# Scores and weighted values of a block in two halves, other TensorE work between the halves, and masks with 32 rows

## The chip, the cores and the metric

One Trainium2 chip; the kernel is one program on one of its cores. The time is device microseconds of that core from start to end, the median of several runs. Lower is better. Engines are named as in the profile: PE is TensorE's matmuls, PEld its weight loads, DVE is VectorE, ACT is ScalarE, POOL is GpSimd, SP issues transfers.

## The reference

Two stages, each inside a layer norm with a residual. The first is an attention over 512 tokens (8 sequences) whose weights are a second-order Taylor expansion of the exponential. The second, which the change touches, is a small transformer of 6 layers:

```python
def attn_layer(x, Wqkv, qs, ksc, Wo):
    q, k, v = jnp.split(x @ Wqkv, 3, -1)          # 16 heads of 64
    q = l2norm(q) * qs
    k = l2norm(k) * ksc
    q = q * cos * scale + rotate_half(q) * sin * scale
    k = k * cos * inv + rotate_half(k) * sin * inv
    out = local_attention(q, k, v)
    return out @ Wo

def local_attention(q, k, v):                     # windows of 32 tokens
    bk2, bv2 = (look(bk), look(bv))               # the window and the one before it
    sim = jnp.einsum('bhwie,bhwje->bhwij', bq, bk2) * QK_SCALE
    sim = jnp.where(mask, -jnp.finfo(sim.dtype).max, sim)
    attn = jax.nn.softmax(sim, -1)
    return jnp.einsum('bhwij,bhwje->bhwie', attn, bv2)

for i in range(DEPTH):                            # 6
    x = attn_layer(shift_tokens(x), ...) + x
    x = ffn_layer(shift_tokens(x), ...) + x       # layer norm, gated GELU, 128 -> 2*341 -> 128
```

All is in float32; tokens are 128 numbers wide.

## The kernel before

**Tiling.** A unit of work is a *block*: 128 tokens (four windows) of one sequence in one layer. There are 6 layers x 8 sequences x 4 blocks = 192. The state of a sequence lies in SBUF by features, so that a projection is a matmul of a block's 128 columns of `state` with 512 columns of weights.

**Stages of a block.** The loop over `t` (line 703) is a pipeline written by hand: in round `t` the functions of block `t`, `t-1`, `t-2` and so on are called in a fixed order, `at(t, lag, step)` calling `step` on block `t - lag`. The steps of a block are:

- lag 0: `proj` for q and then k (two matmuls of 512 columns each, L421, into an `mm` tile in PSUM; VectorE multiplies with the rotary tables, L429 and L436; ScalarE squares both halves, L444; GpSimd adds, L454), `values` (two such matmuls, L481, copied by ScalarE, L482, and spread over windows by transfers into `v2`), `sum_squares` and `unit_length` (reciprocal norms; GpSimd multiplies them in, L470).
- lag 1: `by_features` in two calls (16 transposes of q and k in all; ScalarE copies them into `qT` and `kT`, L514), `scores`: two matmuls (L527) write the mask into both banks of the tile `sp`, and 64 small matmuls (L534: 64 rows, 32 columns of weights, 64 moving columns) add the scores of 16 heads and 4 windows. VectorE takes the maximum (L542), ScalarE does 16 exponentials (L546), VectorE sums them.
- lag 2: `by_keys` (8 transposes of the exponentials, copied into `pT`, L564), `weigh_values` (64 small matmuls, L574, into `po`; VectorE divides, L582), `out_by_features` (8 transposes, copied into `oT`, L596).
- lag 3: `out_project` (8 matmuls, L603, added to `state`, L608).

After the fourth block of a sequence, one step of the feed-forward layer is done in each of the next four rounds: `feed_norm` (4 transposes, layer norm), `feed_first` (4 transposes), `feed_middle` (6 matmuls, GELU, with table loads around it on ScalarE) and `feed_last` (3 matmuls). So of four rounds in a row each has another of these between its second half of `by_features` and its `scores`.

**What sets the order.** Only TensorE's order is fixed by hand (`manual_schedule` for PE, line 694). On the other engines a scheduler puts the instructions in an order when the kernel is built, by its own estimates and by priorities; `tc.high_priority()` stands around the copies out of the transposes, the maximum and the division. [...]

**PSUM.** Tag `mm` has two tiles of two banks, used in turn by q, k, v and the feed-forward matmuls; `tr` two tiles of one bank; `s` a single tile of two banks, which `sp` and `po` share. A new tile on a tag waits until every reader of the tile that it replaces is done. So v's projection waits for all that reads q's, its squares (L444) among it.

A float32 matmul appears in the trace as two records, each with its weight load; 64 small matmuls are 128 records of both kinds.

## Time and profile before

| what | value |
|---|---|
| median of 3 runs | 3888.19 us (3887.2 to 3889.86) |
| the profiled execution | 3893.85 us |
| its span from first to last instruction | 3892.1 us |
| mean granted TensorE clock | 0.99 |
| TensorE records (matmuls, and as many loads) | 65600 |
| second stage: first to last start of a score matmul (L534) | 565.7 to 3847.0 us |

A busy time on PE is not a rate: matmuls overlap, and their ends are modelled. Where the time goes is read from the chain of waits: it is followed back from the last instruction, at each step to what released it. A row such as "L574 PE MATMUL po<-v,pT 64\*32 64x64 f32 x24576 | 299.3, 225 | 44.7" is a group of instructions: line, engine, operation, what it writes from what, rows\*columns of weights, size of the output, number; then its busy time in us, the mean ns of one, and the idle time of the engine just before them with what ended it. In the timeline a row is start, duration, engine, line, operation and count, and in brackets what the engine waited for.

### The profile page before, as it was taken

The numbers are of one execution on the slowest core, as the hardware profiler recorded it, in microseconds if no ns is written. First come the engines' busy times: TensorE is split into PE (matmuls) and PEld (weight loads), VectorE is DVE, ScalarE is ACT, GpSimd is POOL, SyncE is SP. The second block draws the span as 40 slices with busy tenths as digits, with TensorE's granted clock in tenths as the row PEclk, the third lists the DMA queues.
The fourth block names the chain that finished last, engine by engine and source line by source line (L and its number), as shares of the span: only waits on it lengthen the run. The fifth ranks groups of instructions, "written<-read, shape, count | busy, mean of one in ns | idle before, by whom it ended". The sixth has DMA issues, their size and how long they took to land.

```text
span 3892.1 us, 149565 instructions
## 1 busy us (share of the span) xinstructions
PE 3729.8 (96%) x65600; PEld 2474.2 (64%) x65600; DVE 2818.2 (72%) x4300; ACT 2657.5 (68%) x6745; POOL 1837.0 (47%) x1311
## 2 busy tenths in 40 slices
PE   8999989999999999999999999999999999999997
PEld 4555456666666666666666666666666666666665
DVE  4555567777867777777777777777787777777775
ACT  5565656776767777777777677777677777766664
POOL 0000025555555555555555555555555555555552
PEclk9999999999999999999999999999999999999998
DMA  2000012222222222222222322223222222222221
GB/s 81 17 9 12 6 50 71 59 66 60 76 74 63 63 63 66 71 75 65 60 62 64 82 65 66 65 56 82 70 66 59 66 65 56 65 68 68 64 67 37
DMA packets 153208, 233.46 MB, mean 60 GB/s; under 512 B 32622, under 2 KB 53356, under 8 KB 151788
## 3 DMA queue, kind: packets, MB, share of 16 engines
q1 hardware_dynamic: 152556, 223.89, 22.4%
q8 instruction: 517, 8.47, 0.9%
q14 instruction: 135, 1.11, 0.1%
HBM read 24.54 MB, written 4.19 MB: 7 GB/s over the span
## 4 chain that ended last, share of the span: by engine, by line
PE 89%; ACT 5%; issue 3%; DVE 2%; DMA 0%; POOL 0%; POOLq 0%; DVEq 0%; SPq 0%; ACTq 0%
PE tr L70 17%; PE mm L421 17%; PE mm L481 9%; PE py L603 9%; PE sp L534 7%; PE po L574 6%; PE y L282 4%; PE mm L625 3%; PE py L657 3%; PE mm L626 3%; PE sc L252 2%; PE sp L527 2%; ACT sq L444 2%; PE vv L230 2%; PE po L318 2%
## 5 line engine op out<-in xcount | busy, mean ns | idle before, releaser
L454 POOL TENSOR_TENSOR qk<-t,t 128x1024 f32<-128x1024 f32 x384 | 909.2, 2368 | 999.6 <-DVE t L436 999.5
L421 PE MATMUL mm<-wqkv,state 128*128 128x512 f32 x1536 | 727.1, 596 | 3.7 <-ACT v L482 2.6
L470 POOL TENSOR_TENSOR qk<-qk,ss 128x1024 f32<-128x1024 f32 x384 | 722.3, 1902 | 16.0
L429 DVE TENSOR_TENSOR t<-mm,tab 128x512 f32<-128x512 f32 x768 | 497.8, 685 | 242.8 <-PE mm L421 231.3
L546 ACT ACTIVATE pe<-sp,mx 128x64 f32<-128x64 f32 x3072 | 651.4, 376 | 27.6 <-DVE mx L542 27.3
L436 DVE TENSOR_TENSOR t<-mm,tab 128x1024 f32<-128x1024 f32 x384 | 465.9, 1213 | 0.0
L457 DVE TENSOR_REDUCE ss<-sq 128x16 f32<-128x1024 f32 x384 | 461.9, 1203 | 2.0 <-ACT sq L444 2.0
L444 ACT ACTIVATE sq<-mm 128x512 f32<-128x512 f32 x768 | 422.6, 610 | 47.2 <-DVE t L436 45.6
L603 PEld LDWEIGHTS py<-oT,wo 128*128 128x128 f32 x3072 | 374.8, 193 | 93.5 <-issue 56.2
L70 PEld LDWEIGHTS tr<-ident,qk 128*128 128x128 f32 x3072 | 345.7, 141 | 127.1 <-issue 105.7
L70 PE MATMUL tr<-ident,qk 128*128 128x128 f32 x3072 | 412.1, 277 | 7.4 <-ACT qT L514 2.3
L596 ACT COPY oT<-tr 128x512 f32<-128x512 f32 x384 | 207.3, 589 | 266.2 <-PE tr L70 265.2
L421 PEld LDWEIGHTS mm<-wqkv,state 128*128 128x128 f32 x1536 | 264.1, 192 | 191.6 <-issue 188.0
L481 PE MATMUL mm<-wqkv,state 128*128 128x512 f32 x768 | 367.9, 602 | 16.8 <-ACT sq L444 16.8
L603 PE MATMUL py<-oT,wo 128*128 128x128 f32 x3072 | 376.0, 276 | 1.0 <-ACT oT L596 0.9
L582 DVE TENSOR_TENSOR on<-po,su 128x1024 f32<-128x1024 f32 x192 | 235.1, 1224 | 170.1 <-PE po L574 170.1
L534 PEld LDWEIGHTS sp<-kT,qT 64*32 64x32 f32 x24576 | 271.9, 106 | 116.7 <-issue 113.8
L574 PE MATMUL po<-v,pT 64*32 64x64 f32 x24576 | 299.3, 225 | 44.7 <-issue 44.7
L482 ACT COPY v<-mm 128x1024 f32<-128x1024 f32 x192 | 194.5, 1013 | 211.0 <-PE mm L481 211.0
L534 PE MATMUL sp<-kT,qT 64*32 64x64 f32 x24576 | 312.2, 227 | 26.0 <-issue 25.2
L574 PEld LDWEIGHTS po<-v,pT 64*32 64x32 f32 x24576 | 258.5, 105 | 86.4 <-issue 86.2
L542 DVE TENSOR_REDUCE mx<-sp 128x16 f32<-128x1024 f32 x192 | 234.6, 1222 | 106.9 <-PE sp L534 106.3
(108 smaller groups left out, 5171.0 us busy)
## 6 DMA issues: line engine op xcount, KB each, us to landing
v<-v SPq DMA_DIRECT2D x1152, 128.0 KB
v<-v SPq DMA_DIRECT2D x672, 64.0 KB
wqkv<-in_L_ffn_Wqkv_dram SPq DMA_DIRECT2D x6, 1536.0 KB
wo<-in_L_ffn_Wo_dram SPq DMA_DIRECT2D x6, 512.0 KB
xin<-_attn_hidden_states_dram SPq DMA_DIRECT2D x8, 256.0 KB
xr<-_attn_hidden_states_dram SPq DMA_DIRECT2D x8, 256.0 KB
x<-xr SPq DMA_DIRECT2D x8, 256.0 KB
xr<-x SPq DMA_DIRECT2D x8, 256.0 KB
```

The source lines that it names most:

```text
L70: nc.tensor.transpose(ps[:cols, :rows], src, ident[:rows, :rows])
L421: nc.tensor.matmul(ps[:, a].rearrange("p h d -> p (h d)"), lhs, wqkv[:, s, a, :], start=True, stop=True)
L429: nc.vector.tensor_tensor(t2[:, a], ps[:, 1 - a], tab[:, 2 * s + 1, j, HF * a : HF * (a + 1)].unsqueeze(1).to_broadcast([P, H, HF]), ALU.mult,
L436: nc.vector.tensor_tensor(t1, ps, tab[:, 2 * s, j, :].rearrange("p (a d) -> p a d", a=2).unsqueeze(2) .to_broadcast([P, 2, H, HF]), ALU.mult,)
L444: nc.scalar.activation(sq[:, :, a, :], ps[:, a], AF.Square)
L454: nc.gpsimd.tensor_tensor(qk[:, s].rearrange("p h a d -> p a h d"), t1, t2, ALU.add)
L470: nc.gpsimd.tensor_tensor(t, t, ss[:, i, :].unsqueeze(2).to_broadcast([P, H, HD]), ALU.mult)
L481: nc.tensor.matmul(ps[:, p, :], lhs, L["wqkv"][:, 2, p, :], start=True, stop=True)
L534: nc.tensor.matmul(sp[W * w : W * (w + 1), p, pair, :], qT[HD * p : HD * (p + 1), pair, W * w : W * (w + 1)], kT[HD * p : HD * (p + 1), pa ...
L546: ex = nc.scalar.activation(pe[:, pair, p, :], sp[:, p, pair, :], AF.Exp, bias=mx[:, p, pair : pair + 1])
L574: nc.tensor.matmul(po[W * w : W * (w + 1), p, pair, :], pT[r, pair, W * w : W * (w + 1)], v2[r, w, HD * pair : HD * (pair + 1)], start=Tru ...
L603: nc.tensor.matmul(py, L["wo"][:, c, :], oT[:, c, :], start=(c == 0), stop=(c == NP - 1))
```

## The change

Four things are edited.

1. `scores` and `weigh_values` take a half (4 of 8 pairs of heads) and are called twice a round; their ends (maximum and exponentials, division) become `softmax` and `divide`. Between the halves of the scores TensorE now has `out_by_features` and half of the next block's q projection; between the halves of the weighing it has half of v's projection and the first half of `by_features`.
2. `proj` is cut into `project` (one matmul of 512 columns) and `turn` (the work of the other engines), so that a half of a projection can stand alone. The first half of v's projection comes before the weighing, the second within it.
3. The next block's layer is looked up, and loaded if it is new, near the end of the round before.
4. `each` holds, in rows 0 to 31 and again in rows 32 to 63, four 32x32 identities side by side. With it the mask of a block is written by a matmul of 32 rows, taken from rows 0 to 31 for one bank and 32 to 63 for the other. Blocks that begin a sequence keep the 128-row form with `mask0`.

```diff
@@ -65,6 +65,13 @@
 
     mask = const.tile([P, 2 * W], BF16, tag="mask", name="mask")
     mask0 = const.tile([P, 2 * W], BF16, tag="mask0", name="mask0")
+
+    each = const.tile([2 * W, P], BF16, tag="each", name="each")
+    for a in range(2):
+        for w in range(4):
+            nc.vector.tensor_copy(
+                each[W * a : W * (a + 1), W * w : W * (w + 1)], ident[W * a : W * (a + 1), W * a : W * (a + 1)]
+            )
 
     def transposed(ps, src, rows, cols):
         nc.tensor.transpose(ps[:cols, :rows], src, ident[:rows, :rows])
@@ -406,21 +413,25 @@
 
         return dict(wqkv=wqkv, wo=wo, w1=w1, w2=w2, tab=tab)
 
-    def proj(u, s):
+    def project(u, s, half):
+
+        lhs = state[u["b"]][:, u["j"] * P : (u["j"] + 1) * P]
+        if half == 0:
+            u["proj", s] = psum.tile([P, 2, 512], F32, tag="mm", name="mm")
+        nc.tensor.matmul(
+            u["proj", s][:, half, :], lhs, u["L"]["wqkv"][:, s, half, :], start=True, stop=True
+        )
+
+    def turn(u, s):
 
         L, b, j = u["L"], u["b"], u["j"]
-        wqkv, tab = L["wqkv"], L["tab"]
-        lhs = state[b][:, j * P : (j + 1) * P]
+        tab = L["tab"]
         if s == 0:
             u["ss"] = f2.tile([P, 2, H], F32, tag="ss", name="ss")
             u["qk"] = f2.tile([P, 2, H, 2, HF], F32, tag="qk", name="qk")
         ss, qk = u["ss"], u["qk"]
 
-        ps = psum.tile([P, 2, H, HF], F32, tag="mm", name="mm")
-        for a in range(2):
-            nc.tensor.matmul(
-                ps[:, a].rearrange("p h d -> p (h d)"), lhs, wqkv[:, s, a, :], start=True, stop=True
-            )
+        ps = u.pop(("proj", s)).rearrange("p a (h d) -> p a h d", d=HF)
         sq = f2.tile([P, H, 2, HF], F32, tag="sq", name="sq")
         t1 = f2.tile([P, 2, H, HF], F32, tag="t1", name="t1")
         t2 = f2.tile([P, 2, H, HF], F32, tag="t2", name="t2")
@@ -472,14 +483,10 @@
             )
 
     def values(u):
-        L, b, j = u["L"], u["b"], u["j"]
-        lhs = state[b][:, j * P : (j + 1) * P]
+        j = u["j"]
 
         v0 = f3.tile([P, 2, 512], F32, tag="v0", name="v0")
-        ps = psum.tile([P, 2, 512], F32, tag="mm", name="mm")
-        for p in range(2):
-            nc.tensor.matmul(ps[:, p, :], lhs, L["wqkv"][:, 2, p, :], start=True, stop=True)
-        nc.scalar.copy(v0, ps)
+        nc.scalar.copy(v0, u.pop(("proj", 2)))
 
         v2 = f2.tile([P, 4, 512], F32, tag="v2", name="v2")
         for p in range(2):
@@ -516,19 +523,23 @@
             B_["kT"] = f2.tile([P, NP, W + P], F32, tag="kT", name="kT")
             nc.gpsimd.tensor_copy(B_["kT"][:, :, :W], u["kT"][:, :, P:])
 
-    def scores(u):
+    def scores(u, half):
 
         qT, kT = u["qT"], u["kT"]
 
 
-        mk = mask0 if u["j"] == 0 else mask
-        sp = psum.tile([P, 2, NP, 2 * W], F32, tag="s", name="sp", bufs=1)
-        for p in range(2):
+
+        if half == 0:
+            u["sp"] = psum.tile([P, 2, NP, 2 * W], F32, tag="s", name="sp", bufs=1)
+        sp = u["sp"]
+        for p in range(2) if half == 0 else ():
+            r = slice(W * p, W * (p + 1))
+            lhs, mk = (identb, mask0) if u["j"] == 0 else (each[r], mask[r])
             nc.tensor.matmul(
-                sp[:, p], identb, mk.unsqueeze(1).to_broadcast([P, NP, 2 * W]),
+                sp[:, p], lhs, mk.unsqueeze(1).to_broadcast([lhs.shape[0], NP, 2 * W]),
                 start=True, stop=False, skip_group_check=True,
             )
-        for pair in range(NP):
+        for pair in range(NP // 2 * half, NP // 2 * (half + 1)):
             for w in range(4):
                 for p in range(2):
                     nc.tensor.matmul(
@@ -537,6 +548,10 @@
                         kT[HD * p : HD * (p + 1), pair, W * w : W * (w + 2)],
                         start=False, stop=True, skip_group_check=True,
                     )
+
+    def softmax(u):
+
+        sp = u.pop("sp")
         mx = f2.tile([P, 2, NP], F32, tag="mx", name="mx")
         with tc.high_priority():
             nc.vector.tensor_reduce(mx, sp, AX.X, ALU.max, negate=True)
@@ -563,20 +578,25 @@
             with tc.high_priority():
                 nc.scalar.copy(pT[:, c : c + 4, :], ps)
 
-    def weigh_values(u):
-
-        v2, pT, su = u["v2"], u["pT"], u["su"]
-        po = psum.tile([P, 2, NP, HD], F32, tag="s", name="po", bufs=1)
-        for pair in range(NP):
+    def weigh_values(u, half):
+
+        v2, pT = u["v2"], u["pT"]
+        if half == 0:
+            u["po"] = psum.tile([P, 2, NP, HD], F32, tag="s", name="po", bufs=1)
+        for pair in range(NP // 2 * half, NP // 2 * (half + 1)):
             for w in range(4):
                 for p in range(2):
                     r = slice(HD * p, HD * (p + 1))
                     nc.tensor.matmul(
-                        po[W * w : W * (w + 1), p, pair, :],
+                        u["po"][W * w : W * (w + 1), p, pair, :],
                         pT[r, pair, W * w : W * (w + 1)],
                         v2[r, w, HD * pair : HD * (pair + 1)],
                         start=True, stop=True,
                     )
+
+    def divide(u):
+
+        po, su = u.pop("po"), u["su"]
         u["on"] = on = f1.tile([P, NP, 2, HD], F32, tag="on", name="on")
         with tc.high_priority():
             dv = nc.vector.tensor_tensor(
@@ -701,30 +721,35 @@
         for k in range(len(steps) + 2):
             slot(k)
         for t in range(len(units) + 7):
-            if t < len(units):
-                u = units[t]
-                if u["l"] not in layers:
-                    layers[u["l"]] = load_layer(u["l"])
-                u["L"] = layers[u["l"]]
 
 
             gelus = 0 <= t - 5 < len(units) and units[t - 5]["j"] == NB - 1
             if gelus:
                 gelu_only()
-            at(t, 0, proj, 0)
+            if t == 0:
+                units[0]["L"] = layers[0]
+                at(t, 0, project, 0, 0)
+            at(t, 0, project, 0, 1)
+            at(t, 0, turn, 0)
             at(t, 3, out_project)
-            at(t, 0, proj, 1)
+            at(t, 0, project, 1, 0)
+            at(t, 0, project, 1, 1)
+            at(t, 0, turn, 1)
             at(t, 2, by_keys)
 
             if t == 0:
                 head_norm(NG - 1)
+            at(t, 0, project, 2, 0)
+            at(t, 2, weigh_values, 0)
+            at(t, 0, project, 2, 1)
             at(t, 0, values)
             if t == 1:
                 attn_out(B - 1)
             if t == 3:
                 to_state(B - 1)
             at(t, 1, by_features, 0)
-            at(t, 2, weigh_values)
+            at(t, 2, weigh_values, 1)
+            at(t, 2, divide)
             at(t, 0, sum_squares, 1)
             if not gelus:
                 at(t, 0, unit_length)
@@ -735,8 +760,16 @@
             if gelus:
                 at(t, 0, unit_length)
             at(t, 6, feed_last, ends=True)
-            at(t, 1, scores)
+            at(t, 1, scores, 0)
             at(t, 2, out_by_features)
+            if t + 1 < len(units):
+                u = units[t + 1]
+                if u["l"] not in layers:
+                    layers[u["l"]] = load_layer(u["l"])
+                u["L"] = layers[u["l"]]
+                at(t + 1, 0, project, 0, 0)
+            at(t, 1, scores, 1)
+            at(t, 1, softmax)
 
 
 def _rotary(n):
```

## The prediction

> **What bounds the kernel now.** I read the page first (busy times, the chain), then the chain of waits in a stretch of the middle, then the timeline of single blocks, and last what single lines wait for.

> ```profile
> PE 3729.8 (96%) x65600; PEld 2474.2 (64%) x65600; DVE 2818.2 (72%) x4300; ACT 2657.5 (68%) x6745; POOL 1837.0 (47%) x1311
> PE 89%; ACT 5%; issue 3%; DVE 2%; DMA 0%; POOL 0%; POOLq 0%; DVEq 0%; SPq 0%; ACTq 0%
> L574 PE MATMUL po<-v,pT 64*32 64x64 f32 x24576 | 299.3, 225 | 44.7 <-issue 44.7
> q8 instruction: 517, 8.47, 0.9%
> ```

> TensorE makes 89% of the chain that ends last; "issue" is 3% of 3892 us, 117 us. The chain of waits says where that is: inside the two groups of small matmuls.

> ```profile
> 2038.31 0.87 PE tr L70 x8
> 2039.18 1.22 PE po L574 x76
> 2040.40 1.09 issue
> 2041.49 0.43 PE po L574 x24
> ...
> 2056.26 0.87 PE tr L70 x8
> 2057.14 1.72 PE mm L481 x4
> 2058.86 0.87 PE tr L70 x8
> 2059.73 1.42 PE po L574 x91
> 2061.15 1.02 PE tr L70 x8
> ```

> The upper weighing stops for 1.09 us in its middle with no semaphore behind it; the lower runs through in 1.42. A group is 128 loads and 128 matmuls; 8.47 MB of instruction transfers in 517 packets are 16.4 KB each, and for TensorE's 131200 records that is 254 records to a packet. So a group eats about one packet in 1.4 us. These stops, an average 117/192 = 0.61 us a block, are all the idle time there is to win: a block takes (3847.0-565.7)/191 = 17.18 us by the first and last start of L534.

> The other thing to see is what TensorE's third projection (L481) waits for, in a block with a table load (first five lines) and in an ordinary one:

> ```profile
> 2033.89 1.28 ACT L82 ACT_TABLE_LOAD   x1
> 2034.98 1.04 PE L70 MATMUL tr<-ident,pe 128*128 128x128 f32 x8
> 2035.19 1.09 ACT L444 ACTIVATE sq<-mm 128x512 f32<-128x512 f32 x2
> 2036.16 1.08 ACT L564 COPY pT<-tr 128x512 f32<-128x512 f32 x2
> 2036.33 1.98 PE L481 MATMUL mm<-wqkv,state 128*128 128x512 f32 x4 [0.31 <-ACT sq L444]
> ...
> 2055.38 1.09 ACT L444 ACTIVATE sq<-mm 128x512 f32<-128x512 f32 x2 [0.39 <-DVE t L436]
> 2056.10 1.04 PE L70 MATMUL tr<-ident,pe 128*128 128x128 f32 x8
> 2056.74 1.08 ACT L564 COPY pT<-tr 128x512 f32<-128x512 f32 x2 [0.27 <-PE tr L70]
> 2056.97 1.88 PE L481 MATMUL mm<-wqkv,state 128*128 128x512 f32 x4
> ```

> L481 takes the `mm` buffer that the q projection filled, so it may start only when ScalarE has squared both halves of q. In the upper block the squares end at 2036.28 and the matmul starts at 2036.33. In the lower one they end at 2056.47, half a microsecond before TensorE gets there. That half microsecond is the slack on which everything below turns.

> [...] eight transposes occupy 0.87 us before a projection and 1.02 after a weighing. [...] in the first stage eight 32-row records of 384 columns (L252) take 0.86 us, where four full-height records of 512 take 1.91. [...] from 1070 to 1095 us, where TensorE stopped for over 3 us, the granted clock is 0.86, and a q projection lasts 3.41 us instead of 1.88.

> **The change part by part**, per block, in the profiled execution.

> 1. The stops for instructions. Between the halves of the scores now lie eight transposes and half a projection (0.9 + 0.86 us), between the halves of the weighing half a projection and eight transposes: 256 instructions now last over 2.5 us instead of 1.4. I take all of it as gone: -0.61. (Bounds: -0.4 to -0.61.)

> 2. Two more small groups. From the 1.37 us of 114 uninterrupted records (last one 0.22 long) a record takes 10.2 ns, so a half takes 0.65 and the leaving costs 0.15 (1.02 - 0.87); entering costs 0.10 (transposes before a weighing start 0.97 apart from it, 2058.69 to 2059.66, not 0.87). A split adds 0.10 + 0.15[...]: 0.2, two of them +0.4. (0.2 to 0.6.)

> 3. Masks with 32 rows: two matmuls of 0.215 beside each other save 0.215 in three of four blocks (mask0 keeps 128 rows)[...]: -0.12 on average. (-0.16 to +0.05.) The eight small copies that make `each` lie at the start, on VectorE, beside loads: nothing.

> 4. The order on ScalarE. This decides. Nobody wrote it; in the built program it has changed. Before, a block runs: 16 exponentials, both squares of q, both copies of pT, copy of v, and so on (142 of 192 blocks; with a table load behind the exponentials in 46 more). In the changed program those 142 run: 16 exponentials, first square of q, **both copies of pT, second square of q**, both squares of k, qT, kT, copy of v. The 46 run: exponentials, table load, both copies of pT, then all four squares. The first half of v's projection still waits for the second square of q (its semaphore's value is that instruction's), and the pT copies wait for TensorE's transposes of pe. So TensorE finishes those transposes, and has to wait until ScalarE has copied them and then squared q. Behind the waiting matmul stand both weighings, the second half of v, the transposes of q and k, the feed-forward step and the scores.

> Ordinary block, from the first transpose of pe: the eighth ends at 1.04, the second pT copy starts at about 1.08, the square 0.48 later (1.56; two take 1.08), ends 0.60 later (2.16), the matmul starts 0.05 later: 2.21 to 2.24. Without the wait it starts at 0.87. Wait: **1.37**. It cannot be hidden: TensorE's own transposes begin it.

> Table-load block, from the last score matmul: maximum 0.25 to 1.47 (a 1.22 row), exponentials from 1.51 for 3.39 to 4.90, table to 6.20, two copies 1.0 to 7.18, two squares to 8.26, matmul 8.3. TensorE, free of waits, would be there after leaving 0.15, half of q 0.86, L603 1.78, k 1.72 and transposes 0.87: 5.38. Wait 2.93; such a block had 0.47 before: +2.46.

> Block after the feed-forward norm (one of four): its second ScalarE step (exponential of ln_rs) now stands behind both oT copies, which wait for transposes behind the first half of the scores, and VectorE's four xn (0.32 each) all stand ahead of the maximum, where two did. The maximum then starts 0.9 late, and with it the exponentials: wait 2.2 instead of 1.37.

> Smaller: the late start reloads weights, 0.1 in three of four blocks (L481 lasts 1.98 after a wait, 1.88 without); the squares of k now precede the qT copies and wait for VectorE, so the second transposes of q and k start about 0.1 late; the xn transposes wait some 0.3 longer.

> Sum over four blocks: waits 1.37 + 2.2 + 2.46 + 1.37 = 7.4; reloads and late transposes 0.3 + 0.4 + 0.3 = 1.0; splits +1.6; masks -0.5; stops -2.4. Together **+7.1 us per four blocks**, for 48 such fours +341 us. The profiled execution is 3893.85 us; 4235 follows. The median of runs is 5.7 us lower, 4229. To this comes the clock: the 2.9 us waits stand in 46 blocks, and a half-clock window of 3.4 us costs up to 1.7 us; with a sixth of that, some 13 us, I forecast **4240 us**, 9% slower.

> What is moved beside this: loading a layer is issued a third of a block earlier on SP and POOL, with buffers free for a layer: nothing. Half of q earlier: its buffer was read by the squares of k, done 5 us before: nothing. The v copy comes one weighing half later; its transfers are used two blocks on, and have over 20 us: nothing.

> **Rivals.**
> - Faster: the wait is short, because the q buffer is in truth free early and TensorE stays the bound as now. Then -0.61 + 0.4 - 0.12 = -0.33 a block, -63 us: **3825**. For it speaks that L481 waits only 45.9 us in all now (below); against it that the order and the semaphore are in the built program. It decides if the second square of q ends before TensorE's last pe transpose. 7%.
> - Half the wait: ScalarE gets ahead, table-load blocks wait 1.5 and the norm block as others do, splits cost little: four blocks +3.5, +168 us: **4056**. 9%.
> - The clock falls in most table-load blocks and in the norm blocks: 90 windows of 1.2 us, +108 us over 4229: **4337**. 9%.
> - Nothing measurable: stops won and waits lost cancel; it needs waits of 0.3 a block: 3888. 1%.

> ```profile
>   ACT sq L444: 45.9, 93
> ```

> **How the numbers follow.** The forecast has 74%; its own range, from the bounds of the stops, splits and clock and 0.15 us either way on each wait, is 4160 to 4310. For eight in ten I widen it downward and upward: 4110 to 4330. This measurement tells about 0.2% from no change. Slower by more than that: forecast, half wait, clock, 92%; same 1%; faster 7%.

> **What would show it.** Right: the first v matmul of a block (new L421 behind pe transposes) waits for ScalarE's squares (L455), about 1.4 us in most blocks, near 3 in a quarter of them, some 300 us or more in all; the issue share falls to 1% or less; TensorE's busy share falls below 90%; mask pairs start together. Wrong: L421 waits less than 100 us for L455; or "issue" keeps its 3%, and then point 1 fails; or splits show groups of over 0.9 us a half.

## The result, and the profile after

The changed kernel takes **4355.96 us** (median of 4 runs, 4354.68 to 4358.46) against 3887.69 (4 runs, 3883.25 to 3889.86) for the kernel before on the same chip: a ratio of 1.1207, 95% interval 1.1187 to 1.1226. The profiled execution is 4355.78 us with a span of 4354.0, 462 us more than before.

The page of the changed kernel first: the busy times, and the chain that ended last, by engine.

```profile
PE 3947.2 (91%) x65600; PEld 2474.5 (57%) x65600; DVE 2787.1 (64%) x4308; ACT 2637.6 (61%) x6745; POOL 1843.1 (42%) x1311
...
PE 61%; ACT 26%; DVE 10%; issue 2%; DMA 0%; ACTq 0%; POOL 0%; POOLq 0%; DVEq 0%; SPq 0%
```

The same 65600 matmuls, but TensorE's part of the chain has fallen from 89% to 61%, and ScalarE's has risen from 5% to 26%. The mean granted clock is 0.971 where it was 0.99. What TensorE waits for (a line, who lets it go, us in total, times, longest), in the kernel before and in the changed one:

```profile
PE po L574 <- issue: 44.7, 62, 2.1
PE sp L534 <- issue: 25.2, 25, 3.6
PE mm L481 <- ACT sq L444: 16.8, 46, 2.2
PE tr L70 <- ACT qT L514: 14.2, 48, 0.8
```

```profile
PE mm L421 <- ACT sq L455: 323.6, 192, 2.8
PE tr L77 <- ACT qT L521: 17.2, 50, 0.8
...
PE sp L545 <- issue: 4.4, 3, 2.4
```

In all 192 blocks the first half of v's projection waits for ScalarE's squares of q. The stops inside the small groups, which the list puts down to issue and the prediction to instructions, 44.7 and 25.2 us in the kernel before, are 4.4 in the scores and below every row of this list in the weighing. The chain of waits in an ordinary block gives the mechanism piece by piece (start, length, what):

```profile
2041.75 0.81 ACT pe L561 x3
2042.56 0.49 ACT sq L455
2043.05 0.96 ACT pT L579 x2
2044.01 0.51 ACT sq L455
...
2044.56 1.13 PE mm L421 x2
```

Before v starts, the path runs on ScalarE: the last exponentials, a square of q, both copies of pT, and only then the other square. In the kernel before this stretch of the chain was TensorE's own. A block with a table load shows what such a wait does to the rest (timeline: start, length, engine, line, operation; in brackets the idle time before and what ended it):

```profile
3411.57 1.28 ACT L89 ACT_TABLE_LOAD   x1
3412.86 1.07 ACT L579 COPY pT<-tr 128x512 f32<-128x512 f32 x2
3413.82 1.11 ACT L455 ACTIVATE sq<-mm 128x512 f32<-128x512 f32 x2
3414.98 1.13 PE L421 MATMUL mm<-wqkv,state 128*128 128x512 f32 x2 [2.79 <-ACT sq L455]
...
3417.02 2.07 PE L421 MATMUL mm<-wqkv,state 128*128 128x512 f32 x2
3418.89 1.50 PE L77 MATMUL tr<-ident,qk 128*128 128x128 f32 x8
```

After an idle stretch of 2.79 us the half projection at 3417.02 lasts 2.07 us instead of 1.12, and the eight transposes 1.50 instead of 1.04. That is not a wait: the granted clock is 0.77 in the 4 us from 3418 on and 1.00 in the 8 us from 3400 on (windows of time: length; busy time and count of five engines; granted clock; DMA share; GB/s).

```profile
3418.00:3422.00 4.00, 4.00 (x82) 3.08 (x81) 0.78 (x1) 2.19 (x4) 0.70 (x2) 0.77 0.00 0
3400.00:3408.00 8.00, 7.67 (x224) 5.42 (x223) 4.16 (x4) 4.29 (x9) 5.39 (x5) 1.00 0.46 111
```

Counted over the trace, TensorE runs at half clock for 253.6 us, in 68 stretches, 62 of them of 3.41 us; before it was 77.2 us in 16, 12 of them of 3.41 us. Half of the difference, 88 us, is my estimate of the time lost, if TensorE has work throughout.

The idle times of the list are short of the delays, because the modelled end of one group lies behind the start of the next: eight transposes last 1.04 us, and the matmul behind them starts 0.87 after they do. So I count from the start of each group of TensorE to the start of the next, over the second stage. The transposes of the exponentials, behind which v waits, take 191.1 us before and 547.3 after. The 462 us then have these parts:

- the wait before v: +356;
- the two splits, 0.36 us a block each: +138;
- half clock, by the length of the groups that run in it: about +72;
- smaller terms, above all the longer first matmuls of v after a wait: under +10;
- the 32-row masks: about -14;
- the stops that are gone: about -97, more than the 70 of the list, which leaves out gaps under 0.15 us.

The experiments test the main ones.

### The profile page after: what moved, and what is told of

It reads as the page before. It is cut to its first block, busy times and chain, and to the rows that moved or that the text cites. A ratio compares the mean times of both kernels' runs of the same rounds, so it can differ in the third digit from the quotient of the medians.

```text
span 4354.0 us, 149387 instructions
## 1 busy us (share of the span) xinstructions
PE 3947.2 (91%) x65600; PEld 2474.5 (57%) x65600; DVE 2787.1 (64%) x4308; ACT 2637.6 (61%) x6745; POOL 1843.1 (42%) x1311
## 3 DMA queue, kind: packets, MB, share of 16 engines
q8 instruction: 517, 8.47, 0.8%
## 4 chain that ended last, share of the span: by engine, by line
PE 61%; ACT 26%; DVE 10%; issue 2%; DMA 0%; ACTq 0%; POOL 0%; POOLq 0%; DVEq 0%; SPq 0%
PE mm L421 15%; ACT pe L561 12%; PE tr L77 11%; PE sp L545 6%; PE po L590 6%; DVE mx L557 5%; ACT sq L455 4%; ACT pT L579 4%; PE y L289 3%; PE mm L645 3%; PE mm L646 3%; PE py L677 3%; PE sc L259 2%; PE vv L237 1%; PE sp L538 1%
## 5 line engine op out<-in xcount | busy, mean ns | idle before, releaser
L421 PE MATMUL mm<-wqkv,state 128*128 128x512 f32 x2304 | 1269.4, 648 | 326.3 <-ACT sq L455 323.6
L481 POOL TENSOR_TENSOR qk<-qk,ss 128x1024 f32<-128x1024 f32 x384 | 722.2, 1902 | 16.0
L455 ACT ACTIVATE sq<-mm 128x512 f32<-128x512 f32 x768 | 462.3, 636 | 404.8 <-DVE t L447 404.8
L421 PEld LDWEIGHTS mm<-wqkv,state 128*128 128x128 f32 x2304 | 375.8, 197 | 507.4 <-ACT sq L455 368.2
L440 DVE TENSOR_TENSOR t<-mm,tab 128x512 f32<-128x512 f32 x768 | 509.2, 684 | 80.3 <-PE tr L77 74.9
L77 PEld LDWEIGHTS tr<-ident,qk 128*128 128x128 f32 x3072 | 355.6, 145 | 145.3 <-issue 114.3
L590 PEld LDWEIGHTS po<-v,pT 64*32 64x32 f32 x24576 | 279.5, 111 | 197.0 <-issue 196.7
L590 PE MATMUL po<-v,pT 64*32 64x64 f32 x24576 | 346.0, 235 | 0.0
L545 PE MATMUL sp<-kT,qT 64*32 64x64 f32 x24576 | 334.7, 226 | 4.4 <-issue 4.4
L521 ACT COPY qT<-tr 128x512 f32<-128x512 f32 x384 | 232.4, 605 | 51.6 <-PE tr L77 51.6
```

Of the source, the lines that this page charges most:

```text
L77: nc.tensor.transpose(ps[:cols, :rows], src, ident[:rows, :rows])
L421: nc.tensor.matmul(u["proj", s][:, half, :], lhs, u["L"]["wqkv"][:, s, half, :], start=True, stop=True)
L440: nc.vector.tensor_tensor(t2[:, a], ps[:, 1 - a], tab[:, 2 * s + 1, j, HF * a : HF * (a + 1)].unsqueeze(1).to_broadcast([P, H, HF]), ALU.mult,
L455: nc.scalar.activation(sq[:, :, a, :], ps[:, a], AF.Square)
L481: nc.gpsimd.tensor_tensor(t, t, ss[:, i, :].unsqueeze(2).to_broadcast([P, H, HD]), ALU.mult)
L545: nc.tensor.matmul(sp[W * w : W * (w + 1), p, pair, :], qT[HD * p : HD * (p + 1), pair, W * w : W * (w + 1)], kT[HD * p : HD * (p + 1), pa ...
```

## The experiments

My theory after the comparison: (1) v waits because a square of q stands behind the copies of pT in ScalarE's order, (2) the long waits bring half clock, which costs time of its own, (3) each split costs more than I had put on it. The rivals are that the wait comes from splitting itself, since ScalarE's whole path is too long however it is ordered; that the clock is only a companion of the waits; that the splits are nearly free and the waits explain all. The ratio behind each time is against the kernel before, measured beside it on the same chip; two runs from different chips are compared by their times and by their ratios.

**Both squares of q ahead of the copies.** The changed kernel, with one constraint on ScalarE's order (`issue_behind(a, b)` puts `a` behind `b` on their engine):

```diff
-            nc.scalar.activation(sq[:, :, a, :], ps[:, a], AF.Square)
+            squares_of[s] = nc.scalar.activation(sq[:, :, a, :], ps[:, a], AF.Square)
...
-                nc.scalar.copy(pT[:, c : c + 4, :], ps)
+                issue_behind(nc.scalar.copy(pT[:, c : c + 4, :], ps), squares_of[0])
```

> The change, with one thing put back: both squares of q stand ahead of the pT copies on ScalarE, as in the kernel before. Theory ORDER (the wait before v's first half comes from ScalarE's order): exponentials end 4.8 us after the last score matmul, two squares end at 5.7, the matmul starts at 5.8 instead of 6.9; so a wait of 0.4 instead of 1.5 in ordinary blocks, and about 1 us less in the two other kinds. 48 x (4 x 1.05) = 200 us less, and some 50 us less of half clock: about 4100 us. Theory PATH (even in the old order maximum, exponentials and squares are longer than TensorE's work after the second half of the scores) says that a wait for the squares of 0.4 to 2 us stays in every block and that the kernel stays slower than the one before. Theory SPLITS (the doubled small groups cost it): no change, over 4300 us.

Measured: 4152.55 us (4148.03 to 4158.59), ratio 1.0665 (1.0646 to 1.0684), clock 0.991. One constraint takes 203 us off the changed kernel (211 by the two ratios). Its waits:

```profile
PE mm L422 <- ACT sq L456: 141.0, 191, 2.2
PE tr L77 <- ACT qT L522: 49.7, 85, 1.9
```

The idle time before v falls by 183 us, but 191 waits stay, and 33 us come back before transposes of q and k (49.7 for 17.2). Half clock falls to 79 us. So the order is the largest single cause, not the only one.

**The same order given to the kernel before.** Nothing of the change; only a square of q placed behind the copies of pT:

```diff
-            nc.scalar.activation(sq[:, :, a, :], ps[:, a], AF.Square)
+            squares_of[s] = nc.scalar.activation(sq[:, :, a, :], ps[:, a], AF.Square)
...
-                nc.scalar.copy(pT[:, c : c + 4, :], ps)
+                copy = nc.scalar.copy(pT[:, c : c + 4, :], ps)
+        if 0 in squares_of:
+            issue_behind(squares_of.pop(0), copy)
```

> The kernel before in everything, TensorE's order too, save that the second square of q stands behind both pT copies on ScalarE, as in the changed kernel. ORDER alone: v's first matmul comes 2.2 us after the first transpose of pe instead of 0.87 in 142 blocks (+190 us), about 0.9 us later than now in the 46 with a table load (+43 us), the stretches stay under 1.4 us idle so that the clock stays[...]: about 4080 us. If the order is harmless without the halves: 3888 us.

Measured: 4099.76 us (4095.52 to 4102.04), ratio 1.0519 (1.0504 to 1.0534). Without a split and without masks, the order alone costs the kernel before 202 us against the runs beside it (median 3897.68). What TensorE waits for, and in the timeline v's projection in a block without table load:

```profile
PE mm L482 <- ACT sq L445: 238.1, 192, 2.2
PE sp L535 <- issue: 19.2, 20, 3.6
...
PE po L577 <- issue: 2.9, 7, 1.1
```

```profile
2042.72 1.99 PE L482 MATMUL mm<-wqkv,state 128*128 128x512 f32 x4 [1.23 <-ACT sq L445]
```

The wait is 1.23 us, where the kernel before had none. The 202 us are what is left of a larger loss: by the starts of groups the wait costs 245 us, and the weighing is 49 us shorter, because its stops are gone (2.9 us where they were 44.7). So here the stops went with a wait ahead of the group, without any split.

**What the rest of the waiting is.** In the run with the order mended, the first half of the scores stands ahead of the transposes and of half of q, the second half behind them, so the maximum and the exponentials begin later than q's squares would like. Here only the transposes are left between the halves:

```diff
             at(t, 1, scores, 0)
             at(t, 2, out_by_features)
+            at(t, 1, scores, 1)
+            at(t, 1, softmax)
             if t + 1 < len(units):
...
                 at(t + 1, 0, project, 0, 0)
-            at(t, 1, scores, 1)
-            at(t, 1, softmax)
```

> The change with both squares of q ahead of the pT copies, and with only the eight transposes between the halves of the scores; both halves of q follow the second. PATH: what is left of the loss with the old order on ScalarE comes from q's half, 0.86 us of TensorE's work moved ahead of the point where the maximum may begin; without it the waits for the squares fall from 0.45, 1.5, 1.9, 0.45 us (4 blocks) to 0, 0, 0.5, 0. That is 3.8 us in four blocks, 180 us of 4152; stops in the scores come back by some 30 us: about 3950 us. If a wait of 0.4 us or more stays in ordinary blocks, PATH has the wrong place.

Measured: 4013.3 us (4005.63 to 4017.22), ratio 1.0296 (1.028 to 1.0312). That is 139 us less than with half of q in between, and 63 above what I expected. What v waits for:

```profile
PE mm L422 <- ACT sq L456: 51.4, 95, 2.2
```

Only 95 waits are left, in the blocks with a table load and those after the feed-forward norm. By putting 0.86 us of TensorE's work in front of the maximum, the change had lengthened the path from scores to squares by that much.

**Is the clock a cause or a companion?** To the changed kernel I added 141 matmuls whose result is overwritten, just before the waiting half of v: two in rounds with a table load, one in the round after the feed-forward norm. TensorE has more to do; it only idles for a shorter stretch.

```diff
+    def fill(u, n):
+        u["po"] = psum.tile([P, 2, NP, HD], F32, tag="s", name="po", bufs=1)
+        for i in range(n):
+            nc.tensor.matmul(
...
+            if gelus:
+                at(t, 2, fill, 2)
+            elif 0 <= t - 4 < len(units) and units[t - 4]["j"] == NB - 1:
+                at(t, 2, fill, 1)
```

> The change with work added: in the rounds with a table load two matmuls of 512 columns, in the round after the feed-forward norm one, placed in TensorE's order just ahead of v's first half, into the tile of the weighing, which overwrites them. 46 x 2 + 47 x 1 = 139 matmuls of 0.86 us, 120 us of TensorE time, in the place of waiting. Theory CLOCK (the part of the loss over the forecast, some 88 us, is half clock after waits of 1.6 us and more): the idle stretches shrink to below 1 us, the half clock falls from 254 us to below 100, and the kernel gets FASTER by 70 to 90 us: about 4275 us. Without CLOCK: no change or slower, 4356 us or more.

Measured: **4283.67 us** (4280.33 to 4288.62), ratio 1.1003 (1.0987 to 1.1019): 72 us faster than the changed kernel (79 by the two ratios), with more work. What v waits for, and the page's busy times:

```profile
PE mm L421 <- ACT sq L455: 206.8, 192, 2.2
```

```profile
PE 3995.6 (93%) x65882; PEld 2482.5 (58%) x65882; DVE 2787.4 (65%) x4308; ACT 2641.2 (62%) x6745; POOL 1844.8 (43%) x1311
```

The 282 records more than 65600 are the 141 matmuls (the 139 of the expectation were two short). The 117 us fewer of idle time are filled with work and win nothing by themselves. Half clock falls from 253.6 to 82.9 us, 171 us less, half of which is 85. Nor does v start earlier: after the last score matmul it starts at 8.34 us in blocks with a table load and at 7.80 in those after the norm, where the changed kernel has 8.32 and 7.78 (middle cases). So the clock is a cause: 72 to 79 us measured, of some 88 counted.

**The scores in one piece.** The weighing stays split, the masks stay:

```diff
             at(t, 1, scores, 0)
+            at(t, 1, scores, 1)
+            at(t, 1, softmax)
             at(t, 2, out_by_features)
             if t + 1 < len(units):
...
-            at(t, 1, scores, 1)
-            at(t, 1, softmax)
```

> The change with the scores in one piece again, ahead of the transposes and of q's projection; the split weighing, v in two halves and the 32-row masks stay. ORDER and PATH: the wait before v goes back to that of the kernel before (under 60 us in all), the half clock to its 77 us; the stops inside the weighing go (about -60 us), the second small group costs +36, the masks give -29: about 3835 us, faster than the kernel before. SPLITS: half of the loss stays, about 4120 us.

Measured: 3917.05 us (3914.46 to 3917.93), ratio 1.0059 (1.0044 to 1.0074). A miss by 82 us: I had expected a version faster than both. ScalarE's order is that of the kernel before again, and so is the wait before v, 18.2 us where it was 16.8:

```profile
PE tr L77 <- ACT qT L521: 38.5, 49, 0.8
PE mm L421 <- ACT sq L455: 18.2, 51, 2.2
...
PE sp L545 <- issue: 13.2, 11, 4.5
```

So nearly the whole 440 us hang on splitting the scores with half of q between: not by the split's own cost, but by the order and the path that it brings. The miss is in what the split of the weighing costs and what the masks give. Compare starts in ordinary blocks: v, weighing and the first transposes of q and k take 1.72 + 0.97 + 1.41 = 4.10 us before; cut up, 0.95 + 0.79 + 0.96 + 0.97 + 0.79 = 4.46. That is 0.36 us a block, 69 us in all. It is more than the stops that it removes: they fall from 69.9 us in the two small groups to the 13.2 of the scores. And the transposes behind the feed-forward norm wait longer for the copies of qT, 38.5 us where the kernel before had 14.2.

**The weighing in one piece.** The scores stay split:

```diff
-            at(t, 2, weigh_values, 0)
...
+            at(t, 2, weigh_values, 0)
             at(t, 2, weigh_values, 1)
```

(v's two halves thus follow each other again.)

> The change with the weighing, and v ahead of it, in one piece again; the scores stay in halves with q's first half between, and ScalarE keeps copies of pT ahead of the second square. By the run with whole scores a split of the weighing costs 0.37 us a block (71 us) against 60 us of stops, and 0.56 us in a quarter of the blocks. So with ORDER the waits stay as in the changed kernel and the time stays within 60 us of it: 4300 to 4350 us. SPLITS: half of the loss goes, about 4120 us.

Measured: 4286.5 us (4281.63 to 4298.07), ratio 1.1003 (1.0984 to 1.1023): 13 us below the range that I expected. The order of squares and copies and the path are as in the changed kernel:

```profile
PE mm L421 <- ACT sq L455: 324.8, 192, 2.8
...
PE po L590 <- issue: 2.2, 5, 1.0
```

Splitting the weighing costs 69 us here (79 by the ratios), like the 69 worked out from the starts. But TensorE spends 47 us less at half clock, and up to 23 us of the gain come from that, so this run alone does not fix the price of the split. It shows something else: behind the wait the whole weighing has 2.2 us of stops, so in the changed kernel the split was not needed to remove them.

**Only the masks.** The kernel before with 32-row masks:

```diff
+            lhs, mk = (identb, mask0) if u["j"] == 0 else (each[r], mask[r])
             nc.tensor.matmul(
-                sp[:, p], identb, mk.unsqueeze(1).to_broadcast([P, NP, 2 * W]),
+                sp[:, p], lhs, mk.unsqueeze(1).to_broadcast([lhs.shape[0], NP, 2 * W]),
```

> The kernel before with the 32-row masks alone. In the changed kernel the first mask matmul stands 0.32 us ahead of the first score matmul where mask0 has 0.53: 0.21 us in 144 blocks, -30 us if all of it is on the path: 3858 us. If the masks were part of the loss: above 3888.

Measured: 3888.35 us (3884.41 to 3894.68), ratio 0.9986 (0.9976 to 0.9996). A miss: 30 us expected, 5 measured. From the first mask matmul to the first score it is 0.32 us instead of 0.53, as worked out; but the transposes ahead of the masks take 0.08 to 0.10 longer to get there. TensorE's stops:

```profile
PE po L582 <- issue: 48.6, 61, 2.1
PE sp L542 <- issue: 33.1, 45, 3.9
```

They add up to 81.7 us where they were 69.9. Arrived sooner, TensorE stops longer.

**A late table load.** The kernel before with masks, and the table load for the GELU behind the squares of q, so that the 0.47 us wait in a quarter of the blocks goes:

```diff
+        issue_behind(ld, squares_of[0])
...
-            if gelus:
-                gelu_only()
...
+            if gelus:
+                gelu_only()
```

> The kernel before with the 32-row masks and with the table load of a feed-forward round behind both squares of q instead of ahead of them. The 46 waits of 0.47 us before v's projection, and 0.1 us of late weights with each, go: -26 us, -5 for the masks: about 3860 us. If those blocks then wait for something else (the pT copies now stand behind the table load, and the weighing needs them): 3885 us.

Measured: 3894.16 us (3886.75 to 3904.52), ratio 0.9993 (0.9984 to 1.0002). A miss. Against the run with the masks alone, the wait for the squares has fallen from 17.5 us to 3.6, and the stops in the weighing have grown by as much, from 48.6:

```profile
PE po L584 <- issue: 62.8, 60, 2.2
```

**Small groups far apart.** The theory that both expectations call SUPPLY is that closeness of the small groups makes the stops. If so, another order that sets them apart should keep these gains. Two tries, both on the kernel before with masks. In the first, weighing moves up between k and the transposes of q and k, and v moves behind the first of these:

```diff
             at(t, 0, proj, 0)
             at(t, 3, out_project)
-            at(t, 0, proj, 1)
             at(t, 2, by_keys)
+            at(t, 0, proj, 1)
...
-            at(t, 0, values)
+            at(t, 2, weigh_values)
             at(t, 1, by_features, 0)
-            at(t, 2, weigh_values)
+            at(t, 0, values)
```

> The kernel before, with 32-row masks and with TensorE's order in a block changed so that no group of small matmuls follows another closely: q, attention-output product, transposes of the exponentials, k, weighing, first transposes of q and k, v, second transposes, feed-forward steps, scores, transposes of the weighed values. No group is split. Some 4.5 us of long matmuls then lie between weighing and the next scores at least, and 7 us between scores and weighing. Theory SUPPLY [...]: the stops in scores and weighing, some 2.4 us per four blocks above the shortest blocks, go, the share of issue in the chain falls from 3% to below 1%, and with the masks' 0.12 us per block the time is 3770 to 3810 us. Rival SCALAR (the new order makes ScalarE late: it copies the second half of the transposed exponentials behind the squares of q, so weighing waits for it about 0.5 to 1 us in each block): issue falls too, but 190 waits of 0.5 us or more stand in its place, 3880 us or above.

Measured: 4070.69 us (4068.11 to 4073.23), ratio 1.047 (1.0454 to 1.0485). The stops did go, and more came in their place:

```profile
PE tr L77 <- ACT pT L572: 129.9, 143, 1.7
...
PE po L582 <- issue: 10.1, 10, 1.5
...
PE sp L542 <- issue: 7.2, 11, 1.0
```

17.3 us of stops instead of 69.9: with the groups apart the stops are fewer, as the theory had it. But waits for copies of pT and qT and for the addition to the state make up 229.5 us (129.9, 55.3 and 44.3). The transposes of the exponentials now come right behind the attention-output product, whose `tr` tile is still held (timeline of an ordinary block):

```profile
2005.31 1.22 DVE L443 TENSOR_TENSOR t<-mm,tab 128x1024 f32<-128x1024 f32 x1
...
2006.44 0.58 DVE L616 TENSOR_TENSOR state<-py,state 64x128 f32<-64x128 f32 x2
2006.89 0.66 PE L77 MATMUL tr<-ident,pe 128*128 128x128 f32 x4 [0.68 <-ACT pT L572]
```

VectorE adds that product to the state only behind q's rotation, until 2007.0, so the second four transposes wait for the other tile, which a copy of pT frees at 2006.84. The rival that named ScalarE was nearer, but had the wrong place: the 143 waits, 0.9 us on average, are of the transposes, one step ahead of the weighing.

In the second try only v moves, behind the weighing:

```diff
-            at(t, 0, values)
...
             at(t, 1, by_features, 0)
             at(t, 2, weigh_values)
+            at(t, 0, values)
```

> The kernel before, with 32-row masks and with one step moved: v is projected behind the weighing instead of before it. So weighing follows the first transposes of q and k directly, and v (0.9 to 1.4 us of long matmuls) stands between weighing and the second transposes. Nothing is split. Theory SUPPLY: the 0.47 us wait before v for the squares is gone, but weighing's small matmuls now follow the scores 1.4 us sooner, so the stops grow, as in the run with the late table load: 3870 to 3900 us, with issue at 3% or more of the chain. Rival STEP COUNT (the stops have nothing to do with how close the groups stand): the wait goes and nothing comes back, 0.47 us by 190 blocks, 3800 us.

Measured: 4038.97 us (4027.34 to 4043.02), ratio 1.0378 (1.0361 to 1.0395): outside both expectations. The stops in the weighing grow to 82.3 us, and a wait that I hadn't foreseen makes up most of the rest: with v gone from between, the first transposes of q and k catch the `tr` tiles before ScalarE has copied pT out.

```profile
PE tr L77 <- ACT pT L572: 91.7, 191, 1.2
PE po L582 <- issue: 82.3, 46, 2.2
```

None of the ten versions beats the kernel before by more than the 0.14% of the masks alone. Not tried: an order that spreads the groups and also brings the addition to the state ahead of q's rotation.

## Why the prediction was right, and where it failed

The direction, the main cause and the size of that cause were right. The time is 116 us above the forecast and 26 us above the range, because two terms of the sum were each some 60 us too small: the clock and the splits. Either of them put right would have given about 4300 us.

- **Order on ScalarE and the waits: right.** By the prediction's sums v starts 5.38 us after the last score matmul plus a wait of 1.37, 2.2 or 2.93: 6.75 in an ordinary block, 7.58 after the norm, 8.31 with a table load. In the trace the middle cases are 6.89, 7.78 and 8.32. The term was 7.4 us per four blocks, 355 in all; 356 were measured. That the order causes it is shown from both sides, by mending it and by giving it to the kernel before. That both runs moved the time by about 200 us is chance: the first leaves 141 us of waiting, the second has stops that go.
- **Stops in the small groups: right in size, not in the reason.** I put them at 115 us; about 97 went. I had given this to the distance that the splits make. It does work so in the run with whole scores, where the stops of the split weighing are gone with hardly a wait; but two runs have almost none in a whole weighing, the kernel before with the new order (2.9 us) and the change with the weighing in one piece (2.2 us), and both have a wait ahead of it. The issue share of the chain is 2%, not the 1% I named.
- **The clock: the first step that failed.** I wrote that the 2.9 us waits bring half clock in a sixth of cases, 13 us. The trace has 176 us more at half clock, which cost about 72 us, and filling the idle stretches gave back 72. My fault was to reason from one stretch where TensorE had stopped for 3.24 us, as if only a stop of that length counted. Here shorter ones do it. Of the idle stretches ahead of v's projection in the changed kernel, 97 are of about 1.25 us, and none is followed by half clock; of 47 of about 1.6 us 19 are; of 45 of 2.6 to 2.8 us 37. So the waits after the norm, which I had left out, count too, and the longest nearly always do. The last section has further counts.
- **Splits: the second step that failed.** I put 0.4 us a block on the two, with 0.6 as the upper bound; the starts of the groups show 0.36 for each, 0.72. My term had counted entering and leaving once for each split. In the trace the cost is spread over the neighbours too: a half group takes 0.79 us to the next one, two of them 1.58 instead of 1.42, and each half projection beside one takes 0.95 or 0.96 instead of 0.86 (1.06 where it starts after a wait). Over 192 blocks this is 61 us more than forecast.
- **Masks: nearly right.** 0.21 us for the pair and 0.08 to 0.10 for the entry give about 14 us, where I had some 24; in the kernel before the stops swallow most of it.
- **The smaller terms** (reloads, late transposes, 1.0 us per four blocks, 48 us) came out under 10 us. That made up for part of what was missing.
- **The sum.** Four blocks take 68.69 us before and 78.37 after, on average: +9.7, where I had +7.1 and 0.3 for the clock. Without the 1.5 of the clock +8.2 were measured, so the rest of the sum was 1.1 short: 1.3 for the splits and 0.6 for stops and masks, less 0.8 that the smaller terms gave back.
- **The nearest case by luck.** The third rival had the clock's mechanism in the norm blocks too, and its 4337 lies nearest to 4355.96; I gave it 9%. It put 108 us on the clock, where about 72 were measured, and shared the error in the splits; the two partly cancel.
- **TensorE's busy share** is 91%, not below 90%. Busy time rose by 217 us though the matmuls are the same: a matmul at half clock counts longer, and so does a cut projection, whose halves are 1.12 us each where a whole one is 1.88.

## What to carry to other kernels

A new order on one engine makes the scheduler choose new orders on the others, so compare each engine's instructions in both built programs before pricing the edit; here one square behind two copies decided 200 us. In this kernel a wait on TensorE had two prices, its own length and the clock after it: 19 of the 47 idle stretches of about 1.6 us and 37 of the 45 of 2.6 to 2.8 us were followed by half clock, and filler work in them took 72 us off. And small savings ahead of a dense group of small matmuls came back as stops inside it, in the runs with the masks alone and with the late table load.
